# A convolution and attention kernel: another order for the softplus, and other places, queues and times for the first element's loads

## The chip, the cores and the metric

The kernel runs on one core of one Trainium2 chip. Its time is the device time of one execution in microseconds (us). Elements of the batch are called b = 0 to 7.

## The reference, cut to what matters

```python
def reference(x, L0_conv_w1, ..., L1_conv_bv):        # x: (8, 256, 96, 96) float32
    # layer 0: 1x1 convolutions, 2-D Fourier transform, attention over channels in 8 heads, inverse transform, magnitude
    x = x + _L0_conv_ref(_gn(x), ...)
    x = x + _L1_conv_ref(_gn(x), ...)
    return x

def _L1_conv_ref(x, Wq, bq, Wk, bk, Wv, bv):           # xf = x as (b, channel, pixel)
    q = softplus(einsum('dc,bcn->bnd', Wq, xf) + bq)
    k = softplus(einsum('dc,bcn->bdn', Wk, xf) + bk[None, :, None])
    v = einsum('ec,bcn->ben', Wv, xf) + bv[None, :, None]
    attn_map = einsum('bdn,ben->bde', k, v)
    k_sum = sum(k, axis=-1) + EPS
    norm = 1.0 / einsum('bnd,bd->bn', q, k_sum)
    out = einsum('bnd,bde,bn->ben', q, attn_map, norm)
```

`_gn` is a group normalisation. `softplus(z)` is log(1 + exp(z)); the kernel computes it as max(z, 0) + log(1 + e) with e = exp(-|z|), and corrects the logarithm for the rounding of 1 + e.

## The kernel before, in words

All arithmetic is float32. Two arenas of 128 partitions x 2 x 9232 hold an element's image (`x_of(b)`) and its intermediate results (`y_of(b)`); even and odd elements swap them. Each element goes through these stages.

**Pair sums** (`pair_sums`, layer 0). The image is loaded from DRAM in six blocks v = 0 to 5 of 1.5 MB and a small block 6 for the middle row (`load_grouped`: eight DMAs of 192 KB with pieces of two image rows, 768 bytes; nine for block 0, six for block 6). A block has two halves, f and g, and there are two places for blocks, v even and v odd (`staged`). `turn_blocks(u)`, with u = 2v or 2v + 1, copies 16 wrap columns (L364, L365), transposes 32 x 32 squares on DVE (L369) into the one place for turned blocks (`turned`), and after the second half of a block sends it to the DRAM scratch `xtd` (L372, on SP's queue) and asks for block v + 2. `pair(u)` forms sums and differences (L387 to L392, on Pool and DVE) in a ring tile, and `products` feeds PE with them (L343): 12 matmuls a u, in three steps q = 0, 1, 2. So u = 0 to 11 and a last u = 12 give 37 steps, each ended by a `yield`, after one `yield` at the start.

**Rotation** (`rotate`). From i = 22 on, the first element's loop calls `fetch` every second step, which reads `xtd` back, and the table R (`rx`, as tiles `tm`); from i = 27 on, `steps` multiplies the two (L647), 49 steps in all. R is built by `tables()` in the first element only: L266 writes a small table `rt` to DRAM, L270 reads it back spread over 49 rows, L279 and L280 write the result as `rx`. `tables()` then copies `gsel` and other constants on DVE and loads the small weights (`load_small`: 28 DMAs on ACT's queue after a memset of `b12` on Pool). Before, `tables()` is driven by one `next` ahead of the loop and one at each i from 4 on.

**Attention, images** (`attention`, `images`): the rest of layer 0 (L710, L718).

**Layer 1** (`layer1`). The pixels are taken in NS = 6 strips of 4 x 384 columns. For each strip s and c = 0 (k) or 1 (q): 8 matmuls (L812); DVE writes max(z, 0) (L814); ACT writes |z| (L816) and e (L817) into `ex`. Then `softplus(c, s)` has DVE compute u = 1 + e (L834) and the rounding error (L835), ACT the logarithm of u (L836), and DVE the correction (L837); `close` adds the logarithms that are waiting (L843). In the loop over 18 groups i of 128 columns, PE transposes k (`kT`, L867) and the image (`xT`, L878), ACT or DVE copies the latter out of PSUM (L881, L883), and `add_kx` multiplies them (L850), three groups at a time. `den` (L917) follows.

**Output** (`output`) multiplies, adds and stores.

The order of instructions on each engine is that of the program text (`manual_schedule`). Pair sums of the next element are woven into `images`, `layer1` and `output`: `weave(stage, other)` runs one step of the sums for each unit that a stage yields. Tiles of PSUM come from a pool of five (`ps_tile`) and one of three (`acc_tile`).

```python
        for i, _ in enumerate(sums):
            if i > 3:
                next(parts, None)
            if i > 20 and i % 2 == 0:
                fetch()
            if i > 26:
                next(turns)
```

Of the kernel before, what the change touches and what calls it, by code (L numbers as in the profile page):

```python
# [73 lines left out]
def two_layer_kernel(ctx: ExitStack, tc: tile.TileContext, x, w1t, b1, w2t, b2, w3, b3, wot, temp,  # L74
# [32 lines left out]
    def x_of(b):  # L107
        return arenas[b % 2]
# [19 lines left out]
    def staged(b, v, at=0):  # L128

        return x_of(b)[:, v % 2, at * SG:at * SG + SG + at]  # L130

    def turned(b):

        return [x_of(b)[:, c, TO:TO + 2 * NQ * C].rearrange("p (q r n) -> p q r n", q=NQ, r=2) for c in range(2)]

# [25 lines left out]
    nc.scalar.dma_start(out=t0[:, 0:2 * W], in_=tmat[0, :, W:3 * W])  # L161
    for v in range(2):
        load_grouped(0, v)

# [25 lines left out]
    gri = setup[:, 6 * W:6 * W + 2 * P]  # L190
    nc.scalar.dma_start(out=gri, in_=gmat)

    pw = const.tile([P, 1], F32, name="pw")
# [58 lines left out]
    def tables():  # L252
# [9 lines left out]
        for i in range(2):  # L262
            o = (3 + i) * W
            nc.vector.tensor_copy(t0[:, o:o + 1], r0[:, 0:1])
            nc.vector.tensor_copy(t0[:, o + 1:o + W], r0[:, W - 1:0:-1])
        nc.scalar.dma_start(out=rt, in_=t0[:, 3 * W:5 * W])  # L266
        big = y_of(0)[0:W, 1, 0:(N + 1) * (W + 2) + P - W]
        rows = big[:, 0:(N + 1) * (W + 2)].rearrange("p (r w) -> p r w", r=N + 1)
# [66 lines left out]
    def pair_sums(b):  # L335
# [14 lines left out]
        def turn_blocks(u):  # L350

            v, r = divmod(u, 2)
            t = turned(b)
            if u == NG:
                f, g = (staged(b, v, i)[0:W, 0:C].rearrange("p (c w) -> p c w", c=NB8) for i in range(2))
                nc.vector.tensor_copy(g[0:32, :, 31:32], f[0:32, :, 0:1])
                for i, src in enumerate((f, g[:, :, ::-1])):
                    nc.vector.transpose(out=t[i][0:W, 0, 0].rearrange("p (c i) -> p c i", c=NB8), in_=src)
                nc.sync.dma_start(out=xtm, in_=t[0][0:W, 0, 0])
                return  # L360
            f = staged(b, v, 0).rearrange("p (c r w) -> p c r w", c=NB8, r=2)
            if r == 0:
                g = staged(b, v, 1)
                nc.vector.tensor_copy(wrap, g[:, 0:SG:W])  # L364
                nc.vector.tensor_copy(g[:, W:SG + 1:W], wrap)  # L365
            o = SG + (1 - r) * W + 1
            g = x_of(b)[:, v % 2, o:o + SG].rearrange("p (c n) -> p c n", c=NB8)[:, :, W - 1::-1]
            for i, src in enumerate((f[:, :, r], g)):
                nc.vector.transpose(out=t[i][:, :, r].rearrange("p q (c i) -> p q c i", c=NB8),  # L369
                                    in_=src.rearrange("p c (q w) -> p q c w", q=NQ))  # L370
            if r:
                nc.sync.dma_start(out=xtd[:, v].rearrange("c p m -> p c m"), in_=x_of(b)[:, :, TO:TO + 2 * NQ * C])  # L372
                if v + 2 <= NG // 2:
                    load_grouped(b, v + 2)

        def pair(u):

            eo = ring_tile(f"eo_{b}_{u}").rearrange("p (q c n) -> p q c n", q=NQ, c=2)
            nq, np_ = (NQ, P) if u < NG else (1, W)
            ft, gt = (t[0:np_, 0:nq, u % 2] for t in turned(b))  # L380
            e, o = (eo[0:np_, 0:nq, c, 1:C + 1] for c in range(2))
# [288 lines left out]
    def images(b):  # L670
# [53 lines left out]
        for i in range(NC):  # L724
# [35 lines left out]
            if i >= WI:  # L760
                yield 2.5 if i > WI else 1
        for p in pending:
# [6 lines left out]
    def layer1(b):  # L769
# [8 lines left out]
        for k in range(KC):  # L778
            nc.scalar.activation(wkq[:, k], wkq0[:, k], AF.Copy, scale=rstd[:, k:k + 1])
        pb = ps_tile(f"l1b_{b}")  # L780
        for c in range(2):
# [16 lines left out]
        def kq(c, s):  # L798
# [4 lines left out]
            return y_of(b)[:, k, o:o + CH]  # L803

        for s in range(NS):
            n = slice(s * CH, (s + 1) * CH)
            for c in range(2):
# [8 lines left out]
                nc.scalar.activation(ex[:, c, n], ps[:, 0:CH], AF.Abs, bias=bkqs[:, c:c + 1])  # L816
                nc.scalar.activation(ex[:, c, n], ex[:, c, n], AF.Exp, scale=-1.0)  # L817
            if s == 1:
                nmb = own[:, 0:C].rearrange("p (k n) -> p k n", k=KC)
                for k in range(KC):  # L820
                    nc.vector.tensor_scalar_mul(nmb[:, k, :], ones, nmean[:, k:k + 1])
                    nc.vector.tensor_scalar_mul(wvs[:, k, :], wvs[:, k, :], rstd[:, k:k + 1])

        zero = own[:, 5 * C:5 * C + 1]
        nc.scalar.activation(zero, ex[:, 1, NS * CH - 1:NS * CH], AF.Copy, scale=0.0)

        late = []

        def softplus(c, s):

            n = slice(s * CH, (s + 1) * CH)
            z, e = kq(c, s), ex[:, c, n]
            u = two.tile([P, CH], F32, tag="v16", name=f"spu_{b}_{c}_{s}")
            nc.vector.tensor_scalar_add(u, e, 1.0)  # L834
            nc.vector.scalar_tensor_tensor(e, in0=u, scalar=1.0, in1=e, op0=ALU.subtract, op1=ALU.subtract)  # L835
            nc.scalar.activation(u, u, AF.Ln, bias=zero)  # L836
            nc.vector.tensor_sub(z, z, e)  # L837
            late.append((z, u))

        def close():  # L840

            for z, u in late:
                nc.vector.tensor_add(z, z, u)  # L843
            late.clear()
# [11 lines left out]
        pend = []  # L856
        softplus(0, 0)
        yield 2
        pv = ps_tile(f"bvs_{b}")
        for k in range(KC):  # L860
            nc.tensor.matmul(pv[:, 0:C], lhsT=nmb[:, k, :], rhs=wvs[:, k, :], start=(k == 0), stop=(k == KC - 1))
        close()
        nc.vector.tensor_add(bvs, bvs, pv[:, 0:C])
        for s in range(NS):
            pk = ps_tile(f"kT_{b}_{s}")
            for i in range(CH // P):
                nc.tensor.transpose(pk[:, i * P:(i + 1) * P], kq(0, s)[:, i * P:(i + 1) * P], ident)  # L867
            nc.scalar.copy(kq(0, s), pk[:, 0:CH])
            if s + 1 < NS:
                softplus(0, s + 1)  # L870
            for i in range(s * CH // P, (s + 1) * CH // P):
                xt = [slots[2 * (i % 4) + jj] for jj in range(2)]
                for jj in range(2):
                    pt = ps_tile(f"xT_{b}_{i}_{jj}")
# [16 lines left out]
                pend.append((i, xt, kq(0, s)[:, i % (CH // P) * P:(i % (CH // P) + 1) * P]))  # L891
        close()
# [122 lines left out]
    with tc.manual_schedule(engines={E.PE, E.DVE, E.Pool, E.SP, E.Activation}):  # L1015
# [3 lines left out]
        for i, _ in enumerate(sums):  # L1019
            if i > 3:  # L1020
                next(parts, None)
# [66 lines left out]
```

## Time and profile before

| | |
|---|---|
| median of 3 runs | 2661.95 us (2651.09 to 2665.03) |
| the profiled execution | 2650.85 us, of which the span is 2649.0 us |
| busy, share of the span | PE 95%, DVE 68%, ACT 44%, POOL 33% |
| mean clock of PE | 0.984 |
| data moved | 413.27 MB in 282797 packets, 156 GB/s |
| first rotation step, first matmul of `images(0)` | 97.11 us, 178.92 us |
| one softplus stage, L784 to L917 (b = 0) | 349.60 to 406.71 us |

PE, DVE, ACT and POOL are the engines for matmuls, vectors, activations and general work; SP only issues DMAs. PEld is PE's loading of weights. In a timeline a row is: start, us, engine, line, operation, output and input, shapes, count, and in brackets the idle time before it and what ended that. In a list of waits a row is: who waited for whom, us in total, times, longest. In a table of windows: the window, its length, then for each engine the busy time and the number of instructions, the granted clock of PE, the busy share of the 16 DMA engines, and GB/s. L12 is line 12 of the kernel before.

### The profile page before, as it was taken

To read this page: it belongs to the slowest core of one execution; us is meant where nothing else is said; L and a number is where in the kernel's file an instruction comes from. 1 tells how busy PE (TensorE), PEld (TensorE's weight loads), DVE (VectorE), ACT (ScalarE), POOL (GpSimd) and SP (SyncE) were. 2 spreads that over 40 slices of the span, in tenths; PEclk is the share of its full clock that TensorE was granted. 3 is DMA by queue.
4 is the path that set the end of the run, shared out by engine and by line. 5 is a ranking of instruction groups with operands and counts; after the bars stand their busy time and mean duration, and the time that the engine had idled before them with its cause. 6 is when DMAs were issued, how large, how long until landed. Compare 5 with 4: busy or idle time off the path is not lost. (4 is left out here: it accounts for less than half of the span.)

```text
span 2649.0 us, 41157 instructions
## 1 busy us (share of the span) xinstructions
PE 2509.3 (95%) x15580; PEld 1730.2 (65%) x15580; DVE 1789.0 (68%) x3449; ACT 1155.9 (44%) x1985; POOL 865.6 (33%) x817
## 2 busy tenths in 40 slices
PE   3799999999999999999999999999999999999987
PEld 3775666757677576766668566685666757667544
DVE  3457866577756777568675686757866678766766
ACT  0035353453634526344353544435354353534554
POOL 2213514136042451324422343223523135141311
PEclk8899999999999999999999999999999999999999
DMA  9872628637195461935629264492636826286003
GB/s 210 238 216 60 166 71 270 205 67 189 40 313 161 106 173 57 315 120 143 153 90 305 80 167 129 159 316 42 166 89 230 245 60 179 58 289 210 1 7 144
DMA packets 282797, 413.27 MB, mean 156 GB/s; under 512 B 40772, under 2 KB 208872, under 8 KB 282600
## 3 DMA queue, kind: packets, MB, share of 16 engines
q1 hardware_dynamic: 274304, 406.16, 53.2%
q10 hardware_dynamic: 8296, 4.49, 0.8%
q8 instruction: 123, 2.02, 0.3%
q14 instruction: 74, 0.61, 0.1%
HBM read 256.72 MB, written 153.86 MB: 155 GB/s over the span
## 5 line engine op out<-in xcount | busy, mean ns | idle before, releaser
L710 PE MATMUL z<-arena,mz 128*128 128x384 f32 (+1 forms) x2304 | 593.4, 491 | 0.0
L718 PE MATMUL po<-e,wo 128*128 128x384 f32 x1536 | 527.6, 487 | 1.7 <-ACT e L755 1.7
L754 POOL TENSOR_TENSOR e<-e 128x768 f32<-128x768 f32 x192 | 348.4, 1815 | 552.7 <-ACT e L753 529.3
L343 PE MATMUL acc<-eo 128*128 128x257 f32 (+2 forms) x2368 | 437.1, 336 | 50.0 <-POOL eo L382 23.0
L343 PEld LDWEIGHTS acc<-eo 128*128 128x128 f32 (+1 forms) x2368 | 383.8, 194 | 143.9 <-issue 42.4
L710 PEld LDWEIGHTS z<-arena,mz 128*128 128x128 f32 (+1 forms) x2304 | 310.5, 164 | 236.0 <-issue 51.9
L718 PEld LDWEIGHTS po<-e,wo 128*128 128x128 f32 x1536 | 290.0, 190 | 204.7 <-ACT e L755 7.2
L749 DVE TENSOR_TENSOR e<-z,xT 128x768 f32<-128x768 f32 x384 | 361.9, 950 | 75.4 <-PE z L710 74.9
L647 PEld LDWEIGHTS y<-tm,arena 96*128 96x128 f32 x3072 | 365.9, 195 | 52.9 <-issue 18.9
L647 PE MATMUL y<-tm,arena 96*128 96x128 f32 x3072 | 385.7, 281 | 15.3 <-DMA arena<-xtd 6.4
L753 ACT ACTIVATE e<-e 128x1536 f32<-128x1536 f32 x192 | 284.5, 1482 | 195.2 <-DVE e L749 193.3
L391 POOL TENSOR_TENSOR eo<-arena 128x768 f32<-128x768 f32 x88 | 184.5, 2096 | 536.3 <-DVE arena L369 473.2
L720 DVE TENSOR_TENSOR arena<-arena,po 128x384 f32<-128x384 f32 x384 | 209.9, 553 | 190.0 <-PE po L718 190.0
L755 ACT ACTIVATE e<-e 128x768 f32<-128x768 f32 x192 | 162.0, 844 | 367.1 <-POOL e L754 363.2
L986 POOL TENSOR_TENSOR arena<-arena,po 128x384 f32<-128x384 f32 x180 | 179.1, 1014 | 224.0 <-ACT po L985 224.0
L369 DVE STREAM_TRANSPOSE arena<-arena 128x768 f32<-128x768 f32 x192 | 175.7, 953 | 32.5 <-DMA xtd<-arena 23.0
L299 DVE BATCH_NORM_STATS2 st<-arena 128x6 f32<-128x384 f32 x384 | 194.4, 548 | 0.0
L654 ACT COPY ys<-y 128x4 f32<-128x4 f32 (+1 forms) x200 | 32.4, 162 | 363.8 <-DVE arena L653 363.7
L878 PE MATMUL xT<-ident,arena 128*128 128x128 f32 x1152 | 148.4, 277 | 10.0 <-ACT xT L881 9.6
L878 PEld LDWEIGHTS xT<-ident,arena 128*128 128x128 f32 x1152 | 127.2, 142 | 32.0 <-issue 13.6
L985 ACT COPY po<-o 128x384 f32<-128x384 f32 x180 | 79.0, 485 | 157.4 <-PE o L977 152.4
L653 DVE COPY arena<-y 128x384 f32<-128x384 f32 (+1 forms) x200 | 109.1, 546 | 40.8 <-PE y L647 38.6
(225 smaller groups left out, 2493.1 us busy)
## 6 DMA issues: line engine op xcount, KB each, us to landing
xtd<-arena SPq DMA_DIRECT2D x48, 1536.0 KB
arena<-xtd SPq DMA_DIRECT2D x192, 384.0 KB
arena<-in_x_dram SPq DMA_DIRECT2D x96, 768.0 KB
out_dram<-arena SPq DMA_DIRECT2D x192, 384.0 KB
arena<-in_x_dram SPq DMA_DIRECT2D x376, 192.0 KB
tm<-rx SPq DMA_DIRECT2D x96, 159.0 KB
wl<-in_w1t_dram SPq DMA_DIRECT2D x8, 256.0 KB
wl<-in_w2t_dram SPq DMA_DIRECT2D x8, 256.0 KB
```

The lines of the kernel that those rows point to most:

```text
L299: nc.vector.bn_stats(out=st[:, k, c, :], in_=x_of(b)[:, k, c * CH:(c + 1) * CH])
L343: nc.tensor.matmul(acc[c][:, m * (C + 1):m * (C + 1) + C + 1 - m * P], lhsT=eo[0:np_, q, c, 1 + m * P:1 + (m + 1) * P], rhs=eo[0:np_, q, c ...
L391: nc.gpsimd.tensor_add(e, ft, gt)
L647: nc.tensor.matmul(pu[:, o:o + P], lhsT=xt[:, s, k * P:(k + 1) * P], rhs=tm[:, n:n + P], start=True, stop=True)
L710: nc.tensor.matmul(out[:, 0:CH].rearrange("p (h q) -> p h q", q=PR), lhsT=columns(mz, k, c, j), rhs=yz[:, k, f, :, o:o + PR], start=(k == ...
L718: nc.tensor.matmul(po[:, 0:CH], lhsT=wo[:, k, m * P:(m + 1) * P], rhs=e[:, k, :], start=(k == 0), stop=(k == KC - 1))
L720: nc.vector.tensor_add(x[:, m, n], x[:, m, n], po[:, 0:CH])
L749: nc.vector.tensor_add(e[:, 2 * c:2 * c + 2, :].rearrange("p t (q h) -> p t q h", h=H), pz[:, 0:CH].rearrange("p (h q) -> p q h", h=H).uns ...
L753: nc.scalar.activation(e, e, AF.Square)
L754: nc.gpsimd.tensor_add(e[:, 0:2, :], e[:, 0:2, :], e[:, 2:4, :])
L878: nc.tensor.transpose(pt[:, j * C + k * P:j * C + (k + 1) * P], x[:, k, o:o + P], ident)
L986: nc.gpsimd.tensor_add(x[:, m, r], x[:, m, r], t)
```

## The change

Places and loads of the first element: `staged` gives blocks 2 and 3 of b = 0 places of their own; `turned` gives odd blocks of b = 0 a second place, in the other arena. Blocks 0 to 3 are all loaded ahead of the loop, 1 to 3 after the loads of `gavg` and `gmat`; a block that has been turned asks for block v + 4 (block 4 for block 6). The writes to `xtd` of b = 0 are issued from Pool's queue. `tables()` has one more `yield`, after L266, and is driven at i = 3, i = 8 and each i from 9 on.

Softplus, in every element: DVE's three operations become `part(c, s)`, which applies the correction to max(z, 0); for c = 0 they run strip by strip inside the kq loop. `log(c, s)` is ACT's logarithm, in place in `ex`, with 1 as its bias, so that it does not read DVE's u. The ACT copy to `zero` goes. In the loop, `close`, `kT`, the next `log(0, ...)`, `part(1, s)` and `log(1, s)` all stand at the third group of a strip, and DVE takes 12 instead of 6 of the 36 copies. `layer1` has one more `yield`, ahead of L784. (The two forms of the `yield` in `images` give the same values.)

```diff
     def staged(b, v, at=0):
-        return x_of(b)[:, v % 2, at * SG:at * SG + SG + at]
+        o = at * SG + (TO + 2 * NQ * C if b == 0 and v in (2, 3) else 0)
+        return x_of(b)[:, v % 2, o:o + SG + at]
...
+    def turned(b, v):
+        if b == 0 and v % 2:
+            o = H // 2 * W + H // 4 * HB
+            return y_of(b)[:, :, o:o + 2 * NQ * C]
+        return x_of(b)[:, :, TO:TO + 2 * NQ * C]
...
-    for v in range(2):
-        load_grouped(0, v)
+    load_grouped(0, 0)
...
     nc.scalar.dma_start(out=gri, in_=gmat)
+    for v in range(1, 4):
+        load_grouped(0, v)
...
         nc.scalar.dma_start(out=rt, in_=t0[:, 3 * W:5 * W])
+        yield
         big = y_of(0)[0:W, 1, 0:(N + 1) * (W + 2) + P - W]
...
             if r:
-                nc.sync.dma_start(out=xtd[:, v].rearrange("c p m -> p c m"), in_=x_of(b)[:, :, TO:TO + 2 * NQ * C])
-                if v + 2 <= NG // 2:
-                    load_grouped(b, v + 2)
+                (nc.sync if b else nc.gpsimd).dma_start(out=xtd[:, v].rearrange("c p m -> p c m"), in_=turned(b, v))
+                n = v + 2 if b or v + 2 == NG // 2 else v + 4
+                if n < NG // 2 or n == v + 2 == NG // 2:
+                    load_grouped(b, n)
...
             nc.scalar.activation(wkq[:, k], wkq0[:, k], AF.Copy, scale=rstd[:, k:k + 1])
+        yield 1
         pb = ps_tile(f"l1b_{b}")
...
+        def part(c, s):
+            z, e = kq(c, s), ex[:, c, s * CH:(s + 1) * CH]
+            u = two.tile([P, CH], F32, tag="v16", name=f"spu_{b}_{c}_{s}")
+            nc.vector.tensor_scalar_add(u, e, 1.0)
+            nc.vector.scalar_tensor_tensor(u, in0=u, scalar=1.0, in1=e, op0=ALU.subtract, op1=ALU.subtract)
+            nc.vector.tensor_sub(z, z, u)
         for s in range(NS):
...
+            if s:
+                part(0, s - 1)
             if s == 1:
...
-        zero = own[:, 5 * C:5 * C + 1]
-        nc.scalar.activation(zero, ex[:, 1, NS * CH - 1:NS * CH], AF.Copy, scale=0.0)
...
-        def softplus(c, s):
-
-            n = slice(s * CH, (s + 1) * CH)
-            z, e = kq(c, s), ex[:, c, n]
-            u = two.tile([P, CH], F32, tag="v16", name=f"spu_{b}_{c}_{s}")
-            nc.vector.tensor_scalar_add(u, e, 1.0)
-            nc.vector.scalar_tensor_tensor(e, in0=u, scalar=1.0, in1=e, op0=ALU.subtract, op1=ALU.subtract)
-            nc.scalar.activation(u, u, AF.Ln, bias=zero)
-            nc.vector.tensor_sub(z, z, e)
-            late.append((z, u))
+        def log(c, s):
+            e = ex[:, c, s * CH:(s + 1) * CH]
+            nc.scalar.activation(e, e, AF.Ln, bias=ones[:, 0:1])
+            late.append((kq(c, s), e))
...
-        softplus(0, 0)
+        log(0, 0)
+        part(0, NS - 1)
         yield 2
...
-        close()
         nc.vector.tensor_add(bvs, bvs, pv[:, 0:C])
         for s in range(NS):
-            pk = ps_tile(f"kT_{b}_{s}")
...
-            nc.scalar.copy(kq(0, s), pk[:, 0:CH])
-            if s + 1 < NS:
-                softplus(0, s + 1)
             for i in range(s * CH // P, (s + 1) * CH // P):
                 xt = [slots[2 * (i % 4) + jj] for jj in range(2)]
+                if i % 3 == 2:
+                    close()
+                    pk = ps_tile(f"kT_{b}_{s}")
+                    for t in range(CH // P):
+                        nc.tensor.transpose(pk[:, t * P:(t + 1) * P], kq(0, s)[:, t * P:(t + 1) * P], ident)
+                    nc.scalar.copy(kq(0, s), pk[:, 0:CH])
+                    if s + 1 < NS:
+                        log(0, s + 1)
+                    part(1, s)
                 for jj in range(2):
...
-                    if jj or i % 6 > 1:
+                    if jj or i % 3 == 2:
                         nc.scalar.copy(xt[jj][:, :, 0:C], src)
...
-                close()
-                if s >= NS // 2 and i % (CH // P):
-                    softplus(1, 2 * s - NS + i % (CH // P) - 1)
-                if len(pend) == 3:
+                if i % 3 == 0:
                     for p in pend:
                         add_kx(*p)
                     pend = []
+                if i % 3 == 2:
+                    log(1, s)
...
         for i, _ in enumerate(sums):
-            if i > 3:
+            if i in (3, 8) or i > 8:
                 next(parts, None)
```

More of the change, by code (lines that the diff above doesn't have):

```diff
@@ L128, in staged, with mirror, blocks_of @@
     def staged(b, v, at=0):
-        return x_of(b)[:, v % 2, at * SG:at * SG + SG + at]
-    def turned(b):
-        return [x_of(b)[:, c, TO:TO + 2 * NQ * C].rearrange("p (q r n) -> p q r n", q=NQ, r=2) for c in range(2)]
+        o = at * SG + (TO + 2 * NQ * C if b == 0 and v in (2, 3) else 0)
+        return x_of(b)[:, v % 2, o:o + SG + at]
+    def mirror(b, v, o):
+        o += SG + (TO + 2 * NQ * C if b == 0 and v in (2, 3) else 0)
+        return x_of(b)[:, v % 2, o:o + SG].rearrange("p (c n) -> p c n", c=NB8)
+    def turned(b, v):
[3 more added lines that the diff above has]
+        return x_of(b)[:, :, TO:TO + 2 * NQ * C]
+    def blocks_of(b, v):
+        return [turned(b, v)[:, c].rearrange("p (q r n) -> p q r n", q=NQ, r=2) for c in range(2)]
     def load_grouped(b, v):
@@ L352, in turn_blocks @@
             v, r = divmod(u, 2)
-            t = turned(b)
+            t = blocks_of(b, v)
             if u == NG:
@@ L365, in turn_blocks @@
                 nc.vector.tensor_copy(g[:, W:SG + 1:W], wrap)
-            o = SG + (1 - r) * W + 1
-            g = x_of(b)[:, v % 2, o:o + SG].rearrange("p (c n) -> p c n", c=NB8)[:, :, W - 1::-1]
+            o = (1 - r) * W + 1
+            g = mirror(b, v, o)[:, :, W - 1::-1]
             for i, src in enumerate((f[:, :, r], g)):
@@ L379, in pair @@
             nq, np_ = (NQ, P) if u < NG else (1, W)
-            ft, gt = (t[0:np_, 0:nq, u % 2] for t in turned(b))
+            ft, gt = (t[0:np_, 0:nq, u % 2] for t in blocks_of(b, u // 2))
             e, o = (eo[0:np_, 0:nq, c, 1:C + 1] for c in range(2))
@@ L760, in images @@
             if i >= WI:
-                yield 2.5 if i > WI else 1
+                yield 1 if i == WI else 2.5
         for p in pending:
@@ L822, in layer1 @@
                     nc.vector.tensor_scalar_mul(wvs[:, k, :], wvs[:, k, :], rstd[:, k:k + 1])
-        zero = own[:, 5 * C:5 * C + 1]
-        nc.scalar.activation(zero, ex[:, 1, NS * CH - 1:NS * CH], AF.Copy, scale=0.0)
         late = []
-        def softplus(c, s):
-            n = slice(s * CH, (s + 1) * CH)
-            z, e = kq(c, s), ex[:, c, n]
-            u = two.tile([P, CH], F32, tag="v16", name=f"spu_{b}_{c}_{s}")
-            nc.vector.tensor_scalar_add(u, e, 1.0)
-            nc.vector.scalar_tensor_tensor(e, in0=u, scalar=1.0, in1=e, op0=ALU.subtract, op1=ALU.subtract)
-            nc.scalar.activation(u, u, AF.Ln, bias=zero)
-            nc.vector.tensor_sub(z, z, e)
-            late.append((z, u))
+        def log(c, s):
+            e = ex[:, c, s * CH:(s + 1) * CH]
+            nc.scalar.activation(e, e, AF.Ln, bias=ones[:, 0:1])
+            late.append((kq(c, s), e))
         def close():
-            for z, u in late:
-                nc.vector.tensor_add(z, z, u)
+            for z, e in late:
+                nc.vector.tensor_add(z, z, e)
             late.clear()
@@ L861, in layer1 @@
             nc.tensor.matmul(pv[:, 0:C], lhsT=nmb[:, k, :], rhs=wvs[:, k, :], start=(k == 0), stop=(k == KC - 1))
-        close()
         nc.vector.tensor_add(bvs, bvs, pv[:, 0:C])
         for s in range(NS):
-            pk = ps_tile(f"kT_{b}_{s}")
-            for i in range(CH // P):
-                nc.tensor.transpose(pk[:, i * P:(i + 1) * P], kq(0, s)[:, i * P:(i + 1) * P], ident)
-            nc.scalar.copy(kq(0, s), pk[:, 0:CH])
-            if s + 1 < NS:
-                softplus(0, s + 1)
             for i in range(s * CH // P, (s + 1) * CH // P):
                 xt = [slots[2 * (i % 4) + jj] for jj in range(2)]
+                if i % 3 == 2:
[7 more added lines that the diff above has]
+                    part(1, s)
                 for jj in range(2):
```

## The prediction

> **What bounds the kernel now.** I read the busy slices first, then the waits, timeline and DMA view of the first element (0 to 179 us), then the timeline and windows of one later softplus stage.
>
> From the slices of the page (one digit is 66 us):
>
> ```profile
> PE   3799999999999999999999999999999999999987
> DMA  9872628637195461935629264492636826286003
> ```
>
> PE is full from the third slice on, so only PE's own idle time can be won or lost. The start is different: PE stands, and the DMA engines are at 9 and 8. The waits of 0 to 135 us say on what (total us, times, longest):
>
> ```profile
> PE acc L343 <- POOL eo L382: 23.0, 3, 15.1
> DVE wrap L364 <- DMA arena<-in_x_dram: 20.9, 5, 6.0
> DVE arena L369 <- DMA xtd<-arena: 20.4, 4, 7.4
> DVE wrap L364 <- DMA wo<-in_wot_dram: 12.4, 1, 12.4
> SPq L152 <- DMA b<-in_b_dram: 7.5, 1, 7.5
> SPq L154 <- DMA wkq<-in_wkt_dram: 4.6, 1, 4.6
> ```
>
> The first is the end of a chain: Pool waits for the transpose (L369), the transpose for a load or for the write of the last turned block. The SPq rows show that SP's block loads are held until small loads of ACT's queue (b, wkq, wo) have landed: block 2, whose issues begin at 24.71 us, was all there only at 53.45. DMA also has little air, from the windows (us, then PE, PEld, DVE, ACT, POOL busy, clock, DMA share, GB/s; the share passes 1 where reads and writes overlap):
>
> ```profile
> 0.00:97.10 97.10, 45.38 (x220) 39.80 (x221) 36.91 (x91) 2.05 (x5) 26.39 (x80) 0.84 0.90 214
> 97.10:178.90 81.80, 76.48 (x553) 70.53 (x554) 38.86 (x113) 20.41 (x65) 6.66 (x15) 0.92 0.85 246
> ```
>
> The first rotation step runs at 97.11, `images(0)` begins at 178.92. Before 97 PE works 45 us; after it, 76 of 82.
>
> In the softplus stage (here `layer1(0)`; the next six repeat it within 0.2 us) PE is the bound with small holes:
>
> ```profile
> 349.60:365.60 16.00, 16.00 (x224) 6.48 (x224) 7.86 (x16) 12.50 (x23) 2.18 (x4) 1.00 0.34 110
> 365.60:371.00 5.40, 4.29 (x28) 3.57 (x25) 5.09 (x11) 3.85 (x7) 0.83 (x1) 1.00 0.01 3
> 371.00:403.00 32.00, 29.59 (x305) 21.23 (x303) 25.07 (x49) 23.01 (x47) 1.21 (x2) 1.00 0.01 1
> ```
>
> ```profile
> 347.98 0.38 SPq L372 DMA_DIRECT2D xtd<-arena  x1
> 349.60 0.61 PE L784 MATMUL l1b<-nmean_b,wkq 128*32 128x1 f32 x32 [0.93 <-ACT wkq L779]
> 370.52 0.55 PE L867 MATMUL kT<-ident,arena 128*128 128x128 f32 x3 [1.11 <-DVE arena L843]
> 370.71 1.70 DVE L834 TENSOR_SCALAR spu<-arena 128x384 f32<-128x384 f32 x1
> ```
>
> DVE is busy 7.9 of 16 us while PE makes kq (L812), and 25 of 32 us in the kx loop.
>
> **What the Trainium skill says.** "DMA: Bandwidth & Descriptors", section "Issuing engines are not separate DMA queues": transfers of SP, ACT and Pool run on the same 16 engines, another queue saves only issue time; the 0.90 share above agrees. "SBUF — State Buffer", section "SBUF: two separate sides": descriptors of a Pool DMA are written by GpSimd, which a copy-like DVE operation can lock out, and the two also block each other in compute. The second half is seen: L834 took 1.70 us beside Pool's L391 and 0.35 as median. The first half no trace here shows. "TensorE: Matmul & The Clock Gate", section "Part 1: The HAM clock gate": an idle window of about 3.4 us halves the clock. The last element agrees:
>
> ```profile
> 2578.06 0.90 PE L867 MATMUL kT<-ident,arena 128*128 128x128 f32 x3 [3.61 <-DVE arena L843]
> ```
>
> ```profile
> 2578.00:2583.00 5.00, 4.94 (x33) 4.94 (x34) 4.50 (x11) 2.83 (x6) 0.00 (x0) 0.71 0.00 0
> ```
>
> 3.6 us of standing, then a mean clock of 0.71 for 5 us: 1.45 us lost.
>
> **Part A, the first element.** Blocks 0 to 3 now load before the small loads, a turned block no longer waits for the last one's write, and six writes leave SP's queue for Pool's.
>
> Removed: L369's 20.4 us on writes, and most of the hold of block 2. Moved: L270 (1.8 MB in short packets; it landed 19 us after issue at 9.20, sharing with block 1), L279 and L280, and 28 small loads at 0.4 to 0.5 us of issue. On ACT's queue nothing but the loads of the prologue stands ahead of L270, so its new place in the program hardly delays it; only the memset of b12 (behind two more pairs on Pool) holds the small ones. So block 1 still shares with R. With its write now also in flight (issue near 20 us) I let it land at 25 to 27 instead of 24.3.
>
> The floor is bytes. Before the first rotation step there must pass six blocks of 1.57 MB (9.4), three writes (4.7), R and the small loads (4.0), the first fetch (0.5): 18.6 MB. The trace shows 216 GB/s (58 to 97 us) to 275 (16 to 40, reads with writes). At 250 that is 74 us, with 2 us to the first byte 76; at 216, 88. PE alone would be there sooner: start at 16.05, nine u's of 5.2 us, one hole of some 8: 71. Fetch 0 stands in SP's order behind block 5, so it ends the wait. I take 79, a gain of 18. From there PE has 76.5 of 81.8 us of work; two holes of 3.2 us on block reads shrink a little: 2 more. DMA has 20.1 MB left for 80 us, 251 GB/s, about what it did. **A = -20, bounds -10 (step at 87, nothing after) to -28.**
>
> Pool's six issues have no row before (no Pool DMA in it). The DMA page, "Specifications", prices the first byte at about 1 us; I take 1.5 us of Pool each, 9 us in all on an engine busy 26 of 97, behind which stands the next pair's add (L391). From below 0 (SP gains six issues of 0.38 us); from above 3 us each if DVE locks it, 18 us, of which the first delays u=1 by 3 and the rest lie in DMA waits. The twelve gsel copies on DVE (3.4 us) move to u=2, where DVE waits for loads: nothing.
>
> **Part B, softplus, eight times.** Instructions per strip stay: add 0.35, subtract 0.56, subtract 0.56, Ln 0.62, add 0.56; only a 0.20 us ACT copy (L825) goes. Start to start DVE paces them at 0.38, 0.60, 0.48, 0.47, the relu (L814) at 0.54, a copy (L883) at 0.60. What moves:
>
> (1) The new yield runs one sums step (1.4 us of PE) in L784's 0.93 us hole: -0.93. But this step also issues the transposes of u=10, which must wait for the write of the turned block: issued 347.98, and in the DMA view at 300 to 470 GB/s until 353.0. DVE stands from 349.6 to 353.1, then transposes 1.9. Queued behind it are bkqs (L787) and all relus; ACT's Abs follows the relus. PE has five PSUM tiles of 1.29 us and loses only 0.6.
>
> (2) Five `part(0, s)` of 1.46 us now lie between the relus. DVE from 355.0: bkqs 0.2, relus 12 x 0.54, parts 6 x 1.46, tables 1.2, the pair's subtract 0.9, bvs 0.3, two copies 1.2, first close 0.5: 19.6 us plus 0.9 of waits, so kT(0) at 375.5. PE is done with kq at 366.6, steps 2.8, bvs 0.8, two xT groups 1.8: 372.0. It stands 3.5 us, where before it stood 1.1 and then 0.9 (L878).
>
> (3) In the loop each kT follows `close`, which stands on DVE behind the copy of the tile that PE has just filled: 0.15 + 0.60 + 0.55 against PE's next 0.46: 0.96 us lost, five times, 4.8. Against that go the loop's old holes: 32.4 us of span from kT(0) for 27.2 of PE.
>
> Walking both orders in this way to `den` (L917): the old one gives 405.5, with the 1.2 us lock on L834 406.7, the trace has 406.71. The new one gives 409.0, less the 1.4 us of moved step 407.6: +0.9. The 3.5 us stand sits at the clock's edge; half of 1.45 is +0.7. So +1.6 in seven elements, +0.3 in the last, which has no sums: **B = +11.5, bounds 0 (no clock loss, waits as short as before) to +20.** The yield in `images` has the same values in both forms: nothing.
>
> **Sum.** -20 + 11.5 = -8.5, rounded to -8: 2643 for the profiled execution of 2650.85 (span 2649.0 and 1.85 around it). That execution is 11 below the median of 2661.95; the difference goes on the median: **2654**.
>
> **Rivals.**
> - *No change to be seen (my forecast, 0.46).* About 0.5%, 13 us, is what a measurement of this kernel can tell from none. A gains, B gives back; -8, own range 2642 to 2668.
> - *Faster (0.37).* Either A reaches its low bound with B at half (-22, 2640), or the loop keeps the order's promise: DVE no longer waits for Ln inside a strip, PE's holes at L867, L878, L850 (28 us over the eight) and L784 (7.4) all go, and with A the gain is 55: 2607; half of B's holes gives 2627. For it: those waits are real. Against: DVE's 16 us are full.
> - *Slower (0.17).* One mechanism: DVE's backlog ahead of kT(0). If its operations take their listed durations (0.56, 0.62, 0.69), the same walk ends 2.6 us late instead of 0.9, and the stand passes 4 us, with the full 1.45 each time: 4.05 x 7 + 1 = 29, with A's weak end -10: +19, 2681. It decides from 20/7 = 2.9 us per element against A as forecast.
> - *The change does not do what it says:* R is not later, since ACT's queue has nothing else to do. Then small loads still mesh with block 3 and 4; A is -10, the sum +1.5, 2663, within the first case.
>
> The range leaves out the deep end of faster and the far end of slower: **2630 to 2677**.
>
> **What would show it.** Right: first rotation step (L647) at 76 to 87; no L369 wait on xtd before 60 us; L270 issued before 12; in the softplus stage a wait of 3 to 4 us at the first kT, about 1 us at the later ones, a DVE wait of 3 to 4 us on xtd. Wrong: a first step after 92, or kT waits under 0.5 us; then A or B has the other size, and the sum its sign.

## The result, and the profile after

The changed kernel takes **2749.4 us** (median of four runs, 2747.9 to 2753.0), beside 2656.5 for the kernel before on the same chip: ratio **1.0351**, 95% interval 1.0311 to 1.039. It is 93 us slower; the profiled executions differ by 97 (spans of 2746.0 and 2649.0).

The busy slices of the changed kernel's page (one digit is now 69 us) show PE nearly as full as before, and its clock below full:

```profile
PE   3699989999899998999989999999999999899987
...
PEclk8899998999989999899998999899998999989998
DMA  9772627737185462936539164591636826277003
```

With the same 15580 matmuls PE is busy for 2558.3 us instead of 2509.3, so of these 97 us it works half and stands half. From here on I time stages between PE's first instructions on the tiles of each: first rotation step, z sums, l1b, kq, bvs, kT, den, next rotation. Changed kernel less kernel before, summed over the elements:

| stage | difference, us |
|---|---|
| start to first rotation step (97.1 to 109.6) | +12.5 |
| first element's rotation to z sums | -2.4 |
| rotation to z sums, elements 1 to 7 | **+52** |
| z sums to l1b, l1b to kq (with the step added there) | +5 |
| kq to bvs | +11 |
| bvs to den | **+26** |
| den to the next rotation (the step taken away) | -8.5 |

**The first element.** Its waits from 0 to 135 us (total, times, longest):

```profile
DVE eo L408 <- POOL eo L398: 54.5, 5, 30.3
...
PE acc L358 <- POOL eo L398: 50.4, 2, 29.2
POOL xtd L387 <- DMA arena<-in_x_dram: 44.1, 1, 44.1
POOL xtd L387 <- DMA tm<-rx: 23.5, 1, 23.5
```

The transposes' wait for the last write is gone, as the change says. In its place Pool stands 44 and 24 us in front of two of its own writes, waiting for loads. (Some 15 of the 44 it would have stood for the transposes anyway; see first_split below.) Pool's timeline (start, duration, engine, line; the bracket is the idle time ahead) shows what is queued there:

```profile
47.79 0.95 POOL L387 DMA_DIRECT2D xtd<-arena  x1 [44.14 <-DMA arena<-in_x_dram]
48.73 0.14 POOL L398 MEMSET eo<- 128x12 f32 x1
48.96 2.57 POOL L407 TENSOR_TENSOR eo<-arena 128x768 f32<-128x768 f32 x1
...
88.33 0.74 POOL L387 DMA_DIRECT2D xtd<-arena  x1 [23.50 <-DMA tm<-rx]
```

Issuing costs 0.95 and 0.74 us. The price is the place: the next pair's memset and addition stand behind it, DVE's subtraction behind them, and PE 29.2 us behind that.

**The softplus stage.** PE's timeline around the first and second kT:

```profile
385.65 0.87 PE L890 MATMUL kT<-ident,arena 128*128 128x128 f32 x3 [2.99 <-DVE arena L862]
386.31 3.29 PE L900 MATMUL xT<-ident,arena 128*128 128x128 f32 x16
...
392.97 0.52 PE L890 MATMUL kT<-ident,arena 128*128 128x128 f32 x3 [0.90 <-DVE arena L862]
393.33 1.91 PE L900 MATMUL xT<-ident,arena 128*128 128x128 f32 x16
```

Both waits are near the predicted 3.5 and 0.96. After the first, the same transposes take 0.87 for 0.52 and 3.29 for 1.91 us: half clock for one stretch, in every element.

**The rotation.** 17 us from the start of element 1's rotation, first of the kernel before, then of the changed one (us, then busy time of PE, PEld, DVE, ACT, POOL; clock, DMA share, GB/s):

```profile
429.14:446.14 17.00, 16.13 (x116) 11.42 (x114) 9.56 (x29) 7.84 (x21) 8.85 (x11) 0.90 1.03 369
```

```profile
442.71:459.71 17.00, 15.81 (x80) 11.77 (x77) 7.95 (x26) 6.43 (x17) 6.77 (x8) 0.63 0.95 333
```

PE is busy nearly all the time in both, and did 80 instead of 116 matmuls, at a clock of 0.63 instead of 0.90. The stage grows from 67.8 to 69.5 us to 75.8 to 77.3, seven times. It is the largest part of the loss, and the prediction has no line on it.

### The profile page after: what moved, and what is told of

Same layout as the page of the kernel before. It is cut to its first block, busy times and chain, and to the rows that moved or that the text cites. A ratio compares the mean times of both kernels' runs of the same rounds, so it can differ in the third digit from the quotient of the medians.

```text
span 2746.0 us, 41138 instructions
## 1 busy us (share of the span) xinstructions
PE 2558.3 (93%) x15580; PEld 1781.8 (65%) x15580; DVE 1825.6 (66%) x3497; ACT 1131.2 (41%) x1929; POOL 870.8 (32%) x823
## 5 line engine op out<-in xcount | busy, mean ns | idle before, releaser
L663 PEld LDWEIGHTS y<-tm,arena 96*128 96x128 f32 x3072 | 396.9, 208 | 57.8 <-issue 26.3
L663 PE MATMUL y<-tm,arena 96*128 96x128 f32 x3072 | 419.5, 296 | 10.0 <-ACT ys L670 5.0
L669 DVE COPY arena<-y 128x384 f32<-128x384 f32 (+1 forms) x200 | 109.2, 546 | 73.9 <-PE y L663 57.3
L900 PEld LDWEIGHTS xT<-ident,arena 128*128 128x128 f32 x1152 | 136.5, 148 | 17.7 <-issue 16.5
```

What stands on the lines that cost most here:

```text
L663: nc.tensor.matmul(pu[:, o:o + P], lhsT=xt[:, s, k * P:(k + 1) * P], rhs=tm[:, n:n + P], start=True, stop=True)
L900: nc.tensor.transpose(pt[:, j * C + k * P:j * C + (k + 1) * P], x[:, k, o:o + P], ident)
```

## The experiments

Ratios are to the kernel before on the same chip. "Lost" counts the stages from rotation to z sums in elements 1 to 7 that take more than 70 us. This count and the first rotation step are read from one profiled execution of each kernel, the ratio from the medians. The two need not agree: soft_noyield's profiled execution (2686.6 us) is the fastest of its four, at a mean clock of 0.976, and the other three took 2708 to 2717 at 0.964 to 0.969. The one of rec_twice (2702) is the slowest of four, the others took 2691 to 2692. The one of first_only (2676) is the second slowest of twenty with a median of 2664.6.

| kernel | ratio, 95% interval | first rotation step, us | lost |
|---|---|---|---|
| before | 1 | 97.1 | 0 |
| changed | 1.0351 [1.0311, 1.039] | 109.6 | 7 |
| first_only | 1.0034 [1.0018, 1.005] | 110.6 | 0 |
| soft_only | 1.0302 [1.0248, 1.0355] | 97.2 | 6 |
| soft_noyield | 1.019 [1.0129, 1.0252] | 97.7 | 2 |
| yield_only | 1.019 [1.0138, 1.0242] | 96.8 | 7 |
| yield_late | 1.0095 [1.0061, 1.0129] | 98.9 | 2 |
| rec_twice | 1.0143 [1.011, 1.0176] | 98.9 | 7 |
| soft_close | **0.9869 [0.9834, 0.9904]** | 97.9 | 3 |
| first_split | 0.999 [0.9975, 1.0006] | 93.2 | 1 |
| first_r_late | 0.9991 [0.9976, 1.0006] | 98.1 | 0 |
| first_r_gated | 0.9972 [0.9957, 0.9987] | 95.2 | 0 |
| both_mended | 0.9877 [0.9852, 0.9903] | 95.2 | 1 |
| phase_hold | 1.0001 [0.9984, 1.0018] | 94.6 | 6 |
| both_gated | 0.9863 [0.9836, 0.989] | 92.5 | 3 |

### Which part costs what

**first_only** takes the places, Pool's writes and the later R and small loads, and leaves the softplus order of before.

> The kernel before with only the first element's part of the change (places for the blocks, the writes on Pool's queue, R and the small loads later); the softplus order is that of before. Theory 'Pool's queue': the writes of blocks 0 and 2 stand on Pool until the block loads have landed (44 and 24 us in the changed kernel) and hold Pool's additions, so the first rotation step stays at about 109 us as against 97 before, and the whole is 9 to 13 us longer than before (ratio 1.004); every later element has before's stages to 0.1 us. Rival 'the delay comes from elsewhere, such as the softplus order shifting what the planner emits': first rotation step at 79 to 85 us and the whole 15 to 20 us shorter.

The loss of the first element is all there: the first rotation step at 110.6 and the same two waits (0 to 112 us). That every later stage would be before's to 0.1 us did not hold: of the seven rotation stages six take 69.5 us instead of four, and one 67.8 instead of three.

```profile
POOL xtd L387 <- DMA arena<-in_x_dram: 45.2, 1, 45.2
POOL xtd L387 <- DMA tm<-rx: 22.7, 1, 22.7
```

**soft_only** takes the rest.

> The kernel before with only the softplus order and the added step in layer1; the first element is that of before. Both theories expect the rest of the change's loss: +80 to +87 us (ratio 1.031 to 1.034), with +50 in the seven rotation and attention stages and +24 between bvs and the first kT. If the two parts act on each other it would differ from that by over 5 us.

1.0302, and 1.0034 x 1.0302 = 1.0337: the two parts explain the changed kernel's 1.0351 within its interval. Some 80 of the 93 us are softplus order and step.

### The added step, or the softplus order?

**soft_noyield** is soft_only without this line, **yield_only** the kernel before with it alone:

```
+        yield 1
         pb = ps_tile(f"l1b_{b}")
```

> The kernel before with the softplus order alone, without the added step in layer1. Theory 'the moved step': the sums' last step again lies in the output stage just ahead of the rotation, PE's clock is not halved there, the stage from rotation to z sums takes 68 to 69.5 us again instead of 76, and the whole is +30 to +40 us to before. Rival 'the clock falls because the softplus order moves VectorE's and ScalarE's work against the output stage': the stage stays at 75 to 77 us and the whole at +80 us or more, since the step's 1.45 us are back as well.

> The kernel before with the one added step in layer1 and nothing else. Theory 'the moved step': the rotation stage takes 75 to 77 us, +45 to +52 us in seven elements, and the whole is 1.015 to 1.02 of before. Rival 'softplus order': the stage stays at 68 to 69.5 us and the whole is within 10 us of before, on the short side (-6, the pause in layer1 that the step fills).

yield_only fits the theory of the moved step: seven rotation stages at 74.2 to 77.6 us and 1.019. soft_noyield fits only half: five stages at 67.8, but two at 73.9, without the added step, and the whole at +52 us lies between the two expectations. Its slower executions, at a lower clock, probably lost in more stages; they were not profiled. Both alone cost 1.9%, both together 3.0; a sum would be 3.8, but the intervals are too wide to tell 3.0 from it.

**yield_late** keeps the step in layer1, and lets the output stage go without its first sums step instead of its last, so that a sums step again lies ahead of the rotation:

```
                     if 2 * s + m < 4:
-                        next(sums, None)
+                        if s or m:
+                            next(sums, None)
```

> The kernel before with the added step in layer1, and the step that is then missing in the output stage left out at its first place (s, m = 0, 0) instead of its last, so that the last sums step lies just ahead of the rotation as in the kernel before. Theory 'the missing cover': the rotation stage takes 67.8 to 69.5 us again (75.7 in yield_only), at most 1.5 us of stand come at the first output step, and the whole is within 15 us of before. Rival 'the step in layer1 shifts everything against the clock's free-running window': the stage still takes 74 us or more in most elements and the whole is +40 us.

Five of seven stages are back at 67.8 to 68.2 us; two are at 73.9 and 75.4. The ratio of 1.0095 (+25 us) lies outside what either side gave. The cover matters, but it is not all.

**rec_twice** touches neither. It computes four small products of the output stage twice:

```
                 pds = [select(s, ps_tile(f"rec_{b}_{s}")) for s in ss]
+                if ss[0] == 0:
+                    for s, pd in zip(ss, pds):
+                        select(s, pd)
```

> The kernel before, with the four rec products of the output stage's first half computed twice, about 0.9 us more of PE in each of seven elements and nothing else; it moves every later element by a quarter of a 3.4 us window against PE's clock. Theory 'it is the missing step alone': the rotation stage stays at 67.8 to 69.5 us in all elements and the whole is +6 us (+-5). Rival 'it is where the clock's window falls': one to three of the seven elements show a rotation stage of 73 us or more, as two did in soft_noyield, and the whole is +12 to +25 us.

The stage from den to rotation grows by 0.65 us, 4.6 in seven elements. All seven rotation stages are lost (73.9 or 75.5), and the ratio is 1.0143: **4.6 us of work cost 38**. The theory "the missing step alone" falls; the rival named the cause, but its one to three stages and +12 to +25 us were too few.

### Where PE's clock changes

The windows of 0.8 us around one rotation, in the kernel before and in rec_twice (the clock is the third figure from the end):

```profile
753.60:754.40 0.80, 0.54 (x4) 0.54 (x5) 0.80 (x4) 0.38 (x1) 0.80 (x2) 1.00 1.08 401
754.40:755.20 0.80, 0.80 (x8) 0.80 (x7) 0.10 (x2) 0.00 (x0) 0.80 (x2) 0.72 1.07 399
...
757.60:758.40 0.80, 0.80 (x9) 0.10 (x1) 0.00 (x0) 0.00 (x0) 0.00 (x0) 0.65 1.06 399
```

```profile
1087.60:1088.40 0.80, 0.53 (x3) 0.53 (x4) 0.80 (x4) 0.39 (x1) 0.80 (x2) 0.85 1.06 398
1088.40:1089.20 0.80, 0.80 (x6) 0.80 (x5) 0.10 (x1) 0.00 (x0) 0.80 (x2) 0.50 1.06 398
...
1101.20:1102.00 0.80, 0.80 (x7) 0.80 (x6) 0.09 (x1) 0.00 (x0) 0.80 (x2) 0.61 0.00 0
```

The clock is either full or half, so a mean between tells when it changed: 0.72 means full for 0.44 of that window, a fall at 754.75. It rises at 758.16, 3.41 us later; in rec_twice from 1088.16 to 1101.82, 13.66 us, four times 3.41. Read so in every run, all falls and rises of an execution lie on one grid of 3.413 us. In soft_close a fall at 430.29 and a rise at 2024.31 are 467.00 such windows apart.

The Trainium skill ("TensorE: Matmul & The Clock Gate", section "Part 1: The HAM clock gate") says that the gate watches a free-running window of 4096 cycles at 1.2 GHz, 3413 ns. The traces agree with that to 1 part in 10,000. It also says that the clock halves after at least one idle window and comes back after at least one busy one; here the measurement differs. PE stood only 0.54 to 1.08 us of the window ahead of a fall, and the clock stayed at half through four to six windows in which PE was busy nearly all the time.

So I took from each trace the time from the rotation's first step to the next edge of the grid, and set the stage's length beside it. "Ahead" are the 12 kernels with a sums step just ahead of the rotation (84 stages), "missing" the changed kernel, soft_only and yield_only (21):

| to the next edge, us | step ahead: stages, us | step missing: stages, us |
|---|---|---|
| 0.56 to 0.65 | 7: 75.4 to 75.5 | 2: 77.3 |
| 0.67 to 0.90 | 15: 73.9 (one 75.7) | 10: 75.7 to 77.5, one 69.7 |
| 0.95 to 1.14 | 3: 77.0 | 5: 74.2 to 76.1 |
| 1.19 to 1.40 | 19: 69.4 to 69.5 | 1: 77.3 |
| 1.50 to 3.10 | 40: 67.8 to 69.0 | 3 (1.70 to 1.94): 75.7 to 77.6 |

With the step ahead, the place in the window fixes the stage's length almost to a tenth of a us. Without it, every stage seen loses, three of them at places where 40 of 40 others lose next to nothing. Those three are from one execution, and no place beyond 1.94 was met. The cleanest pair is yield_only and yield_late, with the same step added in layer1: at places of 1.66 to 1.94 three stages of yield_only take 75.7 to 77.6 us and four of yield_late, which has a sums step ahead of the rotation, 67.8 to 68.2. So at these places it is the missing step that costs; below 1.15 the step did not save a stage. The first pause of the rotation is also longer there: in yield_only PE is busy 0.19 and 0.63 us of two windows of 0.8, and the step that shortened it is gone.

The pause alone does not decide, though. In the first whole window after the rotation's start PE stood 0.54 to 1.08 us ahead of the 65 falls of the table, and 0.45 to 0.55 us in the 40 stages without one. What separates them better is how much of PE's array was at work. I took for each matmul the rows times the columns of the array that it uses (the `128*32` of a timeline) times the columns moved through it, added this up for every window after the first 150 us in all 15 traces, and set it against the largest sum of any window:

| windows | share of the largest sum |
|---|---|
| first after the rotation's start, clock then falls: 65 | 29% to 37.5% |
| the same, clock stays full: 40 | 37.9% to 53%, one at 37.0% |
| of these, at places 1.66 to 1.94: yield_only (3, falls), yield_late (4, stays) | 29% to 36.7%; 38.7% to 40.1% |
| all at full clock that a fall follows: 203 | 37.8% at most |
| all other at full clock: 10384 | above 37.8%, but for 12 |
| first at half clock in the rotation, clock then back: 20 | 38.3% to 39.2%, one at 36.0% |
| the same, clock stays at half: 45 | 32% to 38.2% |

So an estimate from these traces: the clock goes to half after a window with less than some 38% of the work of the fullest window, and comes back after one with more. It fits why a stage loses one window or several. At half clock a window holds less of the same work, and the rotation, with its matmuls of 96 and 32 rows, then stays below the mark. It fits less well later in a long loss: there windows of 36 to 37% went both ways, and in the nine stages with six windows the last has only 15% to 26%, with matmuls of two columns in it that this sum may count too low. It was worked out afterwards, and no run was made to test it.

**phase_hold** was to use the place in the window. To both_mended (below) it adds seven repeated rec products, to make an element without loss 92.0 windows long.

> both_mended with seven rec products of the output stage computed twice: about 1.35 us more of PE in each of seven elements, so that an element without loss of clock takes 314.1 us, which is 92.0 windows of 3.413 us, and each rotation begins at the same place in a window as the last. Theory 'the place in the window decides': once an element's rotation stage is at 67.8 us all later ones stay there; at most two of seven are above 70, and the whole is within 8 us of both_mended although PE does 9.5 us more. Rival 'the clock's loss in this stage comes from the stage's own work or by chance': elements above 73 us turn up as in soft_close and rec_twice (three to seven of seven), and the whole is 9 us or more above both_mended.

The expectation failed: six stages of seven and 30 us above both_mended are what the rival foretold. But the stages still follow the place. The repeats cost 1.9 us instead of 1.35, and the first rotation of these began at a bad place, 0.73 us ahead of an edge. An element that loses 6.05 us then lasts 320.7 to 321.0 us, which is 94.0 windows, so the next begins at the same bad place. Four stages in a row took 73.9 us; the ratio is 1.0001 where both_mended has 0.9877. All seven stages lie in the rows of the table (which counts them; two of the three in its third row are from here); what I had wrong is which place would be held. The changed kernel does the same: five of its six periods between rotations are 330.9 to 331.5 us, 96.9 to 97.1 windows, and all its stages begin at 0.64 to 1.04. The kernel before has periods of 320.9 us, 94.0 windows, three times, with four stages in a row at 1.2 to 1.4, where the loss is one window at half clock (1.6 us).

### The stand at the first kT

In soft_noyield, VectorE's timeline ahead of the first kT, and PE's line of it:

```profile
370.69 0.56 DVE L811 TENSOR_TENSOR arena<-arena,spu 128x384 f32<-128x384 f32 x1
...
371.58 1.84 DVE L369 STREAM_TRANSPOSE arena<-arena 128x768 f32<-128x768 f32 x2
373.34 0.38 DVE L865 TENSOR_TENSOR own<-own,bvs 128x256 f32<-128x256 f32 x1
373.65 1.28 DVE L888 COPY xT<-xT 128x512 f32<-128x512 f32 x2
374.85 0.95 DVE L845 TENSOR_TENSOR arena<-arena 128x384 f32<-128x384 f32 x1
...
375.94 0.52 PE L873 MATMUL kT<-ident,arena 128*128 128x128 f32 x3 [3.47 <-DVE arena L845]
```

Ahead of the sum that kT needs (L845) stand the last part, the turn, the bias and two xT copies. **soft_close** moves three things there:

```
         log(0, 0)
-        part(0, NS - 1)
         yield 2
+        close()
...
+                if i % 3 == 1:
+                    close()
+                if i == 2:
+                    part(0, NS - 1)
                 if i % 3 == 2:
-                    close()
                     pk = ps_tile(f"kT_{b}_{s}")
```

> The softplus order without the added step, as soft_noyield, with three instructions' places on VectorE changed: the sum that closes k's first piece comes right after the turn (before the bias and the two xT copies), the later ones one tile earlier, and the part of k's last piece after the first kT instead of before the turn. Theory 'the order on VectorE ahead of kT': the stand of 3.47 us at the first kT and the five of 0.9 us vanish, from bvs to den takes 33 to 36 us instead of 40.6 to 43.3 (38.0 before), and the whole is 15 to 40 us shorter than before. Rival 'ScalarE's logarithms are what kT waits for': the waits stay, with ScalarE as the one that releases, and the whole is still above before.

```profile
371.21 1.84 DVE L369 STREAM_TRANSPOSE arena<-arena 128x768 f32<-128x768 f32 x2
373.04 0.56 DVE L845 TENSOR_TENSOR arena<-arena 128x384 f32<-128x384 f32 x1
...
373.75 0.52 PE L876 MATMUL kT<-ident,arena 128*128 128x128 f32 x3 [0.19 <-DVE arena L845]
```

The stand is 0.19 us, one of 0.93 is left of five, and bvs to den takes 33.1 us against 38.0 before and 40.6 to 43.3 in soft_noyield. Three rotation stages lost 6 to 7.6 us; still the ratio is 0.9869. The new softplus order does what it can do once the close stands early: it is **1.3% faster than the kernel before**, clear of the interval, and so faster than the changed one.

### The first element

**first_split** divides each of Pool's writes in two:

```
-  nc.gpsimd.dma_start(out=xtd[:, v].rearrange("c p m -> p c m"), in_=turned(b, v))
+  for c in range(2):
+      nc.gpsimd.dma_start(out=xtd[c, v], in_=turned(b, v)[:, c])
```

> The first element's part alone, as in first_only, with each write on Pool's queue divided into two, one for each half of the turned block, so that the region written no longer spans the addresses of the blocks that are being loaded. Theory 'span of the write': Pool's waits of 45 and 23 us on loads vanish, the first rotation step comes at 76 to 95 us instead of 110.6, and the whole is 2 to 20 us shorter than before (ratio 0.993 to 0.999). Rival 'Pool's queue is the wrong place': the issues themselves, twelve instead of six, or the loads still stop Pool or PE; first rotation step at 100 us or later, ratio 1.000 or above.

Pool's waits on loads vanish; what is left in front of its writes is the wait for the transposes (first 100 us):

```profile
POOL xtd L391 <- DVE arena L384: 20.4, 4, 14.9
```

One write over both halves spans the addresses in between, where blocks are being loaded; each half alone does not. The first step comes at 93.2, as expected, but the whole can't be told from before (0.999). For a new stand comes, of SP's queue (first 100 us), and PE stands 20 us behind it (its timeline):

```profile
SPq L167 <- DMA rx<-arena: 20.2, 1, 20.2
```

```profile
59.27 1.65 PE L358 MATMUL acc<-eo 128*128 128x257 f32 x4 [20.01 <-POOL eo L411]
```

**first_r_late** was to move R's writes later (`if i in (3, 14) or i > 14` for `(3, 8)` and 8).

> first_split, with the third piece of the tables (R's four writes) six sums steps later in the program (i = 14 instead of 8). Theory 'completion counters shared with R': in first_split SP's queue stands 20.2 us on an R write before it can issue block 2's second half, since a load waits for the transfer eight before it, whichever queue issued that; placed later, R's writes no longer stand between the loads, the 20 us stand of PE at 39 to 59 us falls below 8, the first rotation step comes at 76 to 87 us instead of 93.2, and the whole is 6 to 20 us shorter than before. Rival 'the bytes': DMA is full anyway, block 2 comes no earlier than 50 us, the step stays at 90 us or later and the ratio at 0.999.

It did not do what it says: the writes depend on nothing that is later, were issued at the same time (from 32.97 us, 32.89 in first_split), and SP stood 22.3 us on one. **first_r_gated** lets a column of R depend on block 2's turned data:

```
-  nc.scalar.mul(rows[:, :, W + 1:W + 2], csn[0:W, 2, 0:N + 1].unsqueeze(2), -1.0)
   ...
   yield
+  nc.vector.scalar_tensor_tensor(rows[:, :, W + 1:W + 2],
+      in0=x_of(0)[0:W, 0, TO:TO + N + 1].unsqueeze(2), scalar=0.0,
+      in1=csn[0:W, 2, 0:N + 1].unsqueeze(2), op0=ALU.mult, op1=ALU.subtract)
```

> first_r_late, with R's writes made to wait for block 2: the last column of R's rows is written on VectorE from csn plus zero times a piece of block 2's turned data, so that R's writes come after the loads of blocks 1 to 3 in the order of the queues. Theory 'the R write between the loads': SP's stand of 20 to 22 us on an R write is gone, block 2 is there before 45 us instead of 54.8, PE's longest stand after the first is below 10 us instead of 17 to 20, the first rotation step comes at 78 to 90 us instead of 93 to 98, ratio to before 0.992 to 0.998. Rival 'the bytes': the loads issue earlier, but all land later; the stands move to the later blocks or to the first fetch, the step stays at 91 to 98 us and the ratio at 0.998 to 1.001.

SP's longest stand on an R write is 5.4 us now, but it stands 19.2 us on R's large load instead, and PE's longest stand in the sums is still 14.0 us. PE has done nearly all its sums by 80, and then stands 15.6 us for the first fetch, which SP issues behind the last loads (these wait 5.8 us on a small load, bkq). The first step at 95.2 is the rival's; the ratio, 0.9972, leaves 7 us of gain, and of these three it is the only one whose interval leaves out 1. Two windows of this kernel:

```profile
0.00:80.00 80.00, 44.81 (x220) 39.29 (x220) 38.38 (x90) 1.92 (x4) 32.27 (x90) 0.85 1.04 245
80.00:95.17 15.17, 0.00 (x0) 0.03 (x1) 2.12 (x4) 0.00 (x0) 0.00 (x0) 0.64 0.68 190
```

and the time up to the first rotation step in first_split:

```profile
0.00:93.20 93.20, 46.18 (x220) 40.10 (x220) 38.57 (x93) 2.05 (x5) 32.19 (x90) 0.84 0.97 240
```

93.2 us at 240 GB/s are 22.4 MB, and the share is 0.97. The rival "the bytes" fits in all three: whichever stand goes, some 22 MB lie ahead of the first fetch, the DMA engines have little air, and another stand takes its place. It was not tested by taking bytes away. Nor do these first steps differ by much more than executions do: the three kernels with first_r_late's first element have 98.1, 95.2 and 94.6.

### Both together

**both_mended** is soft_close with first_r_late's first element, **both_gated** with first_r_gated's.

> soft_close with first_r_late's first element. If the two parts add, the ratio to before is that of soft_close (0.987) less what first_r_late gains (0.003 to 0.007): 0.979 to 0.985, with bvs to den at 33.1 us in seven elements and the first rotation step as in first_r_late. Two to four elements may lose 6 us in the rotation stage, as three did in soft_close.

> both_mended with the R writes of first_r_gated. If the first element gains, the whole is 5 to 15 us below both_mended and soft_close (ratio to before 0.980 to 0.985); if the bytes are the floor there, it is within 6 us of them (0.985 to 0.990). Rotation stages by the place in the clock's window: two of seven or fewer above 73 us.

0.9877 and 0.9863: no different from soft_close's 0.9869 within the intervals. So both_mended missed its 0.979 to 0.985, both_gated fell where "the bytes" put it, and lost in three stages instead of two. The first element adds nothing that can be told apart.

## Why the prediction was wrong

The forecast was 2654, no change to be seen; it is 2749. By its steps:

- **Part A, -20: measured +10.** Two steps failed. "I take 1.5 us of Pool each" priced the issue (0.95 and 0.74 measured) and not what the issuing engine waits for before it: 44 and 24 us, with the next pair's addition behind. And the floor of 18.6 MB was mis-sized: it counted three writes, but in the kernel before four were issued ahead of the first fetch and in first_split five. The kernel before had moved 20.8 MB by its first step (97.1 us at the 214 GB/s of the prediction's own line), first_split 22.4. So the mended first elements have their first rotation step at 92.5 to 98.1 us, against 96.8 to 98.9 in the seven kernels with the old one, and not 18 us earlier. The sign of being wrong that was named, a first step after 92, came true. The weak bound of -10 was not weak enough: a loss had been left out.
- **R hardly delayed by its new place: right.** R's large load issues at 8.92 us (9.20 before), since nothing holds ACT's queue.
- **The kT waits: right in mechanism and size.** 3.0 us (3.5 in soft_noyield) and 0.9 at the later ones, for 3.5 and 0.96. The rival "slower by DVE's backlog ahead of kT(0)" named the right place.
- **"half of 1.45 is +0.7", and +0.9 for the walk to den: too small.** The clock halves at this stand in each of the seven elements, and costs one window at half speed, 1.7 us. Without that, in the elements of soft_noyield that kept full clock, bvs to den still takes 40.6 us for 38.0. Both together cost 3.5 to 3.8 us an element; 26 in all.
- **The yield, -0.93 in the hole less 0.6: the 0.6 is mis-sized.** From kq to bvs PE takes 1.1 to 3.1 us more, in yield_only 1.2 to 2.8, and in soft_noyield nothing. That is more than the hole had to give. The wait of DVE ahead of its transposes is 1.7 us, half of the 3 to 4 predicted, and in the profile it ends with a block's load and not with the write.
- **The step taken from the output stage, -1.4: this is where most of it failed.** The sum counted 1.4 us of work fewer and asked nothing of what this step had covered. Without it PE's clock is at half for 17 or 20.5 us in each rotation: +52. A clock price was set on long stands only, after the last element's 3.6 us, and none on the rotation; here the clock fell after windows in which PE stood 0.8 to 1.1 us. That a shift in time alone can cost as much, as in rec_twice, was on no list of rivals either.

What of the +52 is the missing step and what the place in the window can be divided only roughly. At the places where the changed kernel's stages began, 0.65 to 1.04, kernels with the step take 73.9 to 77.0 us; by the table about 40 of the 52 us (an estimate) would have been lost there with the step in place. But the step also helps to set the place, and yield_only loses at places that are good for all others. That the work in a window decides, as the shares above suggest, stays untested. Other versions of the rotation's order were not tried.

## What to carry to other kernels

An instruction that issues a DMA from a compute engine's queue costs that engine all that the transfer waits for, so look up what it waits for and which region its one access pattern spans. Before a filler, a piece of work that covers a pause, is moved out of a stage, ask what PE's activity in that stage will be without it, and read the clock by stages, not the share of busy time. In a loop whose period is near a whole number of clock windows, a small change can cost many times its size (here 0.65 us an element cost eight times as much); judge an edit by stages that lie apart from that, and by several neighbours of it.

## What the runs showed of the hardware that I had not expected

- The clock's edges keep one grid of 3.413 us through an execution, and with the sums step in place the length of the rotation stage follows from its place on it (84 stages, table above). A loss that is repeated can lock the loop to the place that causes it (93.97 and 97.0 windows).
- The clock fell after windows in which PE stood 0.54 to 1.08 us, and stayed at half for up to six windows (20.5 us in element 2 of first_split) while PE was busy. Rows times columns times moved columns separate the windows with a fall (at most 37.8% of the fullest) from the others better than PE's standing time does.
- 4.6 us of added PE work made the kernel 1.43% slower.
